# A graph layer's edge sums: gathers counted as landing later, and more sums fed to the matmul in two parts

## The chip, the cores and the metric

One core of a Trainium2 chip runs the whole kernel in one launch. The metric is the time of the device in microseconds (us); the median of three runs stands for a kernel. TensorE (PE) multiplies matrices and puts the result into PSUM, VectorE (DVE) and ScalarE (ACT) work on rows of 128 partitions, GpSimd (POOL) issues the gathers (indirect DMAs), and SyncE (SP) issues the plain DMAs. Each engine takes its instructions strictly in the order in which they were written; across engines they wait for one another by semaphores.

## The reference

A relational graph layer over 625 nodes of 512 features, 20625 edges sorted by destination, 4 kinds of edges. What matters, with the norms written as functions:

```python
h   = relu(layernorm(x))
msg = sum over r of (h[src] @ W_rel[r] + b_rel[r]) * where(type == r, weight, 0)
agg = segment_sum(msg, dst) / max(segment_sum(weight, dst), 1)
x1  = layer_norm(h + h @ W_self + b_self + agg)
out = x + layer_norm(x1 + gelu(x1 @ W_ffn1 + b_ffn1) @ W_ffn2 + b_ffn2)
```

All of it is float32. The kernel computes h @ W_rel[r] for all nodes and kinds first (the table), so that an edge's message is one row of the table, times its weight.

## The kernel before

The nodes lie in five blocks of 128 rows. The first 84 us make the table: 20 chunks of 128 rows (4 kinds by 5 blocks), each four float32 matmuls, stored to DRAM. The first and the last block (the outer ones) take their messages from dense products of the chunks with small matrices of summed weights; for that, chunks are loaded back from DRAM (L1297, SP) into three buffers of two chunks, and multiplied (L1302, PE). For the three inner blocks the rows are gathered edge by edge, and this is where the change lies.

A gather (L1159, POOL) fetches 128 rows of the table, one per partition, into one of ten buffers "ms". There are 99 of them. The first eight and the last one are single tiles, whose rows go straight to a matmul. The other 90 are 30 groups of three tiles in which the edges of one partition have the same destination, so the three rows can be added before the matmul: ScalarE takes the first row times its weight into one of two PSUM buffers "add" (L1165), VectorE adds the second and third (L1183). Then the group's sum goes to TensorE with a matrix of ones and zeros "oh" that picks the destination, and TensorE accumulates all groups of a run in "acc". Six further gathers (L1216, "x_row"), two for each inner block, fetch the edges of a node that share a group with the node before; VectorE adds them to the block's sums itself (L429). A run is the stretch of tiles that fall into the same block, or into the same two neighbours. By their groups the five runs with groups have 8, 2, 9, 2 and 9 of them; I number the groups 1 to 30 in this order. The last run also has the last single tile.

The sum of a group gets to TensorE in one of two ways. Whole: VectorE's last add writes it to a buffer "es", and TensorE multiplies it in float32 (L1208), which takes two passes. In two parts ("parted", or split): ScalarE casts the sum to a shorter format, "eh" (L1169), VectorE takes the rest, "el", by subtraction (L1173), and TensorE multiplies each in one fast pass (L1205, L1206).

When a run is complete, VectorE adds "acc" to the block's row sums z (L429); a block with all its parts is normalised (L880 to L892), turned by TensorE (L351) and copied by ScalarE (x1T, L1363). Then comes its feed-forward: eight up-projections (L928, 16 of the profile's matmul instructions for every two of them), each followed by a gelu on ScalarE (L932), eight down-projections (L946), the second norm on VectorE (L956 to L971, with root steps L862 to L869) and the store. The feed-forwards run in the order first outer, last outer, then the three inner blocks; by this order I speak of the fourth block (the second inner one) and of the last block (the third inner one). Self products of a block's own rows (L441) and sums over outer tiles (L613) fill in between. After the last run's sums TensorE may do dummy matmuls, the spins (L1226), at the lowest rank.

All of this, from the first gather on, is put into order by a planner (class Plan, L76). Each step is registered with an engine, a duration, the steps it comes after and the buffers it takes and gives back; the planner plays the steps through with these numbers and writes the instructions in the order in which they started in that play. Nothing else of the numbers reaches the chip. Two of them matter here. A gather takes 1.26 and counts as landed 3.6 (LAND) after that, plus an extra by its index n among the 99 gathers (LATE, L1258): the first pair of the table whose bound exceeds n gives the extra. And `parted` (L1175) says which groups go in two parts.

Of the kernel before, what the change touches and what calls it, by code (L numbers as in the profile page):

```python
# [154 lines left out]
def gnn_layer(ctx, tc, x, edges, edge_line, edge_groups, w_self, w_rel, w_ffn1, w_ffn2, rows_in, bf1_in, out, n_edges):  # L155
# [852 lines left out]
    SUM = 3  # L1008
    WARM = 24
    ES = 7  # L1010
    LAND, LATE = 3.6, ((8, 2.0), (40, 1.2))
    HOTS_AT, SELF_AT, ADDS_AT = (15, 16, 17), 15, (16, 17, 18)
    OHS = 3
    OW = 5
# [1 line left out]
    GATHER = 1.26  # L1016
    SLACK = 1.2
    LATER = 0.3
    PARTED = 1, 1
    BEHIND = 5  # L1020
    CELLS = 3.0
    FIRST_PIECE = 4
# [102 lines left out]
    order_of = sorted(of_sum, key=lambda bs: (not set(bs) & set(OUTER), -bs[0] if set(bs) & set(OUTER) else bs))  # L1125
# [37 lines left out]
    def first_row(j, ms, box):  # L1163
        box["sum"] = buffer("add")
        nc.scalar.activation(box["sum"], ms[j], AF.Copy, scale=wgt[:, j:j + 1])  # L1165

    def high(j, box):
        box["high"] = edge.tile([P, D], F32R, tag="es", name=f"eh_{j}", bufs=ES)
        nc.scalar.copy(box["high"], box["sum"])  # L1169

    def low(j, box):
        box["low"] = edge.tile([P, D], F32R, tag="es", name=f"el_{j}", bufs=ES)
        nc.vector.tensor_sub(box["low"], box["sum"], box["high"].bitcast(F32))  # L1173

    def parted(k, units):  # L1175
        return len(units[k]) > 1 and k % PARTED[1] < PARTED[0] and k + 3 < len(units)

    def row_added(j, ms, box, parts):
        k, q = divmod(j - GROUP0, EG)
        to = box["sum"]  # L1180
        if q == EG - 1 and not parts:
            to = edge.tile([P, D], F32, tag="es", name=f"es_{j}", bufs=ES)
        nc.vector.scalar_tensor_tensor(to, ms[j], wgt_g[:, k, q - 1:q], box["sum"], op0=ALU.mult, op1=ALU.add)  # L1183
        box["sum"] = to
# [46 lines left out]
    for bs in order_of:  # L1231
        tiles = of_sum[bs]
        units = []
# [13 lines left out]
        for k, unit in enumerate(units):  # L1247
# [15 lines left out]
            for q, (j, g) in enumerate(zip(unit, got)):  # L1263
                alone, whole = len(unit) == 1, q == len(unit) - 1
                if alone:
                    h = g
                elif q == 0:
                    h = row0 = op("ACT", 0.69, lambda j=j, box=box: first_row(j, ms, box), after=[g],
                                  take=["add"], give=[("ms", g)], lag=SLACK, rank=rank)
                else:  # L1270
                    parts = parted(k, units)
                    h = op("DVE", 0.75, lambda j=j, box=box, parts=parts: row_added(j, ms, box, parts), after=[g, h],
                           take=["es"] if whole and not parts else [],
                           give=[("ms", g)] + ([("add", row0)] if whole and not parts else []), lag=LATER, rank=rank)
                    h_last = h
                    if whole and parts:
                        h = op("ACT", 0.65, lambda j=j, box=box: high(j, box), after=[h], take=["es"], rank=rank)
                        h = op("DVE", 0.7, lambda j=j, box=box: low(j, box), after=[h], take=["es"], give=[("add", row0)], lag=0.6, rank=rank, level=0.7)
            end = unit is units[-1]
            parts = parted(k, units)  # L1280
            m = op("PE", 0.47 if parts else 0.87,
                   lambda bs=bs, k=k, q=k - k0, end=end, ohs=ohs, box=box, j=unit[0]: edge_sum(bs, k, q, end, ohs, box, j),
                   after=[h, hots_op, m], take=["acc"] if k == 0 else [],
# [290 lines left out]
```

## Time and profile before

| | |
|---|---|
| median of three runs | 260.74 us (260.15 to 263.15) |
| the profiled execution | 262.26 us, its span 260.5 us |
| granted TensorE clock, mean | 0.993 |
| busy: TensorE, VectorE, GpSimd, ScalarE | 95%, 77%, 66%, 29% of the span |
| gathers of L1159 | 99, the first at 88.1 us, the last at 221.7 us |

In a row of the timeline stand start, duration, engine, line, operation, what is written and read, the count, and in brackets the idle time of the engine just before, with what ended it. A float32 matmul is two instructions in the counts. The durations of neighbouring instructions overlap a little, since an engine begins one while the one before drains; where it matters, the time from start to start is used. In a group's row (a line, engine and operation) stand the count, the busy time, the mean in nanoseconds, and the idle time ahead. In a row by windows stand the stretch, its length, busy time and count of each engine in the order PE, weight loads, DVE, ACT, POOL, then granted clock, DMA share and GB/s.

### The profile page before, as it was taken

Reading aid. Unit: us, or ns where it says so; the run is one execution under the profiler, and the core shown is the slowest. Engines: PE = TensorE matmul, PEld = TensorE weight load, DVE = VectorE, ACT = ScalarE, POOL = GpSimd, SP = SyncE. Lnnn points to the kernel's source line nnn. Section 1 sums busy time; section 2 is a strip of 40 time slices with the busy share of each in tenths; the row PEclk is TensorE's granted clock in tenths of the full one; section 3 lists DMA queues with packets and bytes.
Section 4 is the critical chain, followed back from the end, with each engine's and each line's share of the span. In section 5 each row is a group of like instructions: output and inputs, shape, how many; then the busy total and the mean of one; then the engine's idle time right before and its main releaser. Section 6 shows DMA issues by size and latency. Waiting matters only on the chain. (4 is left out here: it accounts for less than half of the span.)

```text
span 260.5 us, 3515 instructions
## 1 busy us (share of the span) xinstructions
PE 246.4 (95%) x1051; PEld 141.4 (54%) x1051; DVE 200.5 (77%) x503; ACT 74.8 (29%) x224; POOL 172.0 (66%) x230
## 2 busy tenths in 40 slices
PE   8899999999999969999959999989999998899996
PEld 6444444445445625443424444864685964675964
DVE  2896999997979964839879399997798985973614
ACT  3017300000031573623121142641223632310420
POOL 4478889887888577777778777777777777100000
PEclk9999999999999999999999999999999999799999
DMA  5999999972272599799997977777776677330101
GB/s 191 361 402 416 379 382 360 321 285 81 73 253 85 199 363 328 227 346 299 367 325 219 374 232 201 218 191 208 213 212 205 199 204 213 111 110 6 44 0 44
DMA packets 24055, 60.20 MB, mean 231 GB/s; under 512 B 4401, under 2 KB 8753, under 8 KB 22882
## 3 DMA queue, kind: packets, MB, share of 16 engines
q0 software_dynamic: 9936, 27.58, 35.0%
q1 hardware_dynamic: 13808, 30.94, 32.1%
q10 hardware_dynamic: 290, 1.44, 1.6%
q8 instruction: 9, 0.15, 0.2%
q14 instruction: 12, 0.10, 0.1%
HBM read 50.77 MB, written 9.17 MB: 230 GB/s over the span
## 5 line engine op out<-in xcount | busy, mean ns | idle before, releaser
L1159 POOL DMA_INDIRECT ms<-table,row_i x99 | 97.2, 982 | 30.8 <-issue 13.4
L403 PE MATMUL ps<-wr,hT 128*128 128x512 f32 (+2 forms) x168 | 71.2, 576 | 0.0
L686 POOL DMA_INDIRECT cells<-weight,cell x45 | 48.6, 1080 | 9.0 <-issue 6.4
L403 PEld LDWEIGHTS ps<-wr,hT 128*128 128x128 f32 x168 | 30.6, 190 | 33.8 <-issue 29.9
L1183 DVE SCALAR_TENSOR_TENSOR add<-ms,wgt_g,add 128x512 f32<-128x512 f32 x48 | 35.7, 748 | 16.8 <-DMA ms<-table,row_i 14.9
L928 PEld LDWEIGHTS ps<-x1T,w_sb 128*128 128x128 f32 x320 | 39.1, 197 | 5.2 <-issue 3.2
L928 PE MATMUL ps<-x1T,w_sb 128*128 128x128 f32 (+1 forms) x320 | 39.7, 281 | 0.9 <-ACT gT L932 0.9
L1165 ACT ACTIVATE add<-ms,ed 128x512 f32<-128x512 f32 x30 | 20.7, 692 | 66.5 <-DMA ms<-table,row_i 47.3
L946 PE MATMUL ps<-w_sb,gT 128*128 128x512 f32 (+3 forms) x96 | 36.2, 522 | 0.0
L1302 PE MATMUL acc<-tr,sums_w 128*128 128x512 f32 x60 | 27.7, 595 | 0.0
L599 ACT ACTIVATE ohw<-os,w 128x128 fp32r<-128x128 f32 x36 | 11.4, 389 | 56.3 <-DVE os L581 55.3
L946 PEld LDWEIGHTS ps<-w_sb,gT 128*128 128x128 f32 (+1 forms) x96 | 16.6, 188 | 14.4 <-issue 11.8
L932 ACT ACTIVATE gT<-ps,bf 128x128 f32<-128x128 f32 (+1 forms) x40 | 13.3, 362 | 19.6 <-PE ps L928 14.9
L441 PE MATMUL ps<-ws_sb,hT 128*128 128x512 f32 x40 | 18.3, 592 | 0.0
L1302 PEld LDWEIGHTS acc<-tr,sums_w 128*128 128x128 f32 x60 | 11.0, 190 | 12.3 <-issue 11.2
L1208 PE MATMUL acc<-es,oh 128*128 128x512 f32 x24 | 12.9, 626 | 3.2 <-DVE es L1183 3.2
L416 DVE SCALAR_TENSOR_TENSOR tr<-ps,rx,brel_bc 128x512 f32<-128x512 f32 x15 | 11.2, 744 | 3.3 <-POOL idle L689 2.1
L1173 DVE TENSOR_TENSOR el<-add,eh 128x512 fp32r<-128x512 f32 x18 | 12.3, 681 | 0.9 <-ACT eh L1169 0.8
L1169 ACT CAST eh<-add 128x512 fp32r<-128x512 f32 x18 | 10.5, 581 | 8.2 <-DVE add L1183 8.2
L956 DVE TENSOR_TENSOR ow<-ps,z 128x512 f32<-128x512 f32 (+3 forms) x6 | 3.6, 599 | 11.4 <-PE ps L946 11.3
L441 PEld LDWEIGHTS ps<-ws_sb,hT 128*128 128x128 f32 x40 | 7.6, 190 | 8.7 <-issue 8.6
L1205 PE MATMUL acc<-eh,oh 128*128 128x512 f32 x18 | 11.7, 651 | 0.0
(215 smaller groups left out, 302.5 us busy)
## 6 DMA issues: line engine op xcount, KB each, us to landing
tr<-table SPq DMA_DIRECT2D x11, 512.0 KB, 6.3
w_sb<-in_L_gnn_W_ffn_dram SPq DMA_DIRECT2D x2, 2048.0 KB, 9.5
table<-tr SPq DMA_DIRECT2D x15, 256.0 KB, 6.3
wr<-in_L_gnn_W_rel_dram SPq DMA_DIRECT2D x3, 1024.0 KB, 8.8
cells<-zeros SPq DMA_DIRECT2D x2, 1280.0 KB, 12.5
ms<-table,row_i POOLq DMA_INDIRECT x99, 3.8
rows<-in_rows_dram SPq DMA_DIRECT2D x1, 1536.0 KB, 13.0
sums_w<-cells ACTq DMA_DIRECT2D x1, 1280.0 KB, 5.9
```

Of the source, the lines that this page charges most:

```text
L403: nc.tensor.matmul(p_[:, :h.stop - h.start], hT[i][:, k, :], wr_sb[r][:, k, h], start=(k == 0), stop=(k == KD - 1))
L441: nc.tensor.matmul(p[0], hT[i][:, k, :], ws_sb[:, k, :], start=(k == 0), stop=(k == KD - 1))
L686: s = nc.gpsimd.indirect_dma_start(out=cells[i][:, :], out_offset=bass.IndirectOffsetOnAxis(ap=cell[i][:, k:k + 1], axis=0), in_=weight[i] ...
L928: nc.tensor.matmul(pu[:, :nn], w1_sb[:, k, f * P:(f + 1) * P], x1T_b()[:, k, :nn], start=(k == 0), stop=(k == KD - 1))
L932: nc.scalar.activation(box["gT"][:, f, :nn], pus[f][:, :nn], AF.Gelu, bias=bf1[:, f:f + 1])
L946: nc.tensor.matmul(po[h][:n, :w], box["gT"][:, f, at], w2_sb[:, f, c], start=(f == 0), stop=(f == KF - 1))
L1159: nc.gpsimd.indirect_dma_start(out=ms[j], out_offset=None, in_=table[:, :], in_offset=bass.IndirectOffsetOnAxis(ap=row_i[:, j:j + 1], axis=0))
L1165: nc.scalar.activation(box["sum"], ms[j], AF.Copy, scale=wgt[:, j:j + 1])
L1173: nc.vector.tensor_sub(box["low"], box["sum"], box["high"].bitcast(F32))
L1183: nc.vector.scalar_tensor_tensor(to, ms[j], wgt_g[:, k, q - 1:q], box["sum"], op0=ALU.mult, op1=ALU.add)
L1208: nc.tensor.matmul(acc[bs], ohs[0][:, q, :].bitcast(F32), box["sum"] if "sum" in box else ms[j], start=(k == 0), stop=last)
L1302: nc.tensor.matmul(acc[b,], sums_w[b][:, c, :], kept[(b, c) if (b, c) in kept else c], start=first, stop=last)
```

## The change

Two settings of the layout, and the rule for split sums:

```diff
-    LAND, LATE = 3.6, ((8, 2.0), (40, 1.2))
+    LAND, LATE = 3.6, ((8, 3.5), (56, 2.5), (120, 0.5))
...
-    PARTED = 1, 1
+    PARTED = 2, 3
...
-    def parted(k, units):
-        return len(units[k]) > 1 and k % PARTED[1] < PARTED[0] and k + 3 < len(units)
+    def parted(bs, k, units):
+        return len(units[k]) > 1 and k % PARTED[1] < PARTED[0] and (k + 3 < len(units) or bs != order_of[-1])
...
-                    parts = parted(k, units)
+                    parts = parted(bs, k, units)
...
-            parts = parted(k, units)
+            parts = parted(bs, k, units)
```

LATE: the first eight gathers now count as landing 3.5 later than LAND instead of 2.0, those up to the 40th 2.5 instead of 1.2, those from there to the 56th 2.5 instead of nothing, and the rest, up to the 99th, 0.5 instead of nothing. The x_row gathers keep LAND alone.

PARTED: before, every group is split, other than the last three members of its run. Now the first two of every three groups of a run are split, and the last three members are left whole only in the last run (bs is the run's blocks, order_of[-1] the last run).

Both change the order that the planner writes out. Three places follow, on which the prediction rests.

TensorE, near the end of the first run of groups (the fifth to eighth group's sums, into acc_1); before:

```order
L1205 MATMUL acc_1_1174<-eh_1229,oh_1190 128x512
L1206 MATMUL acc_1_1174<-el_1263,oh_1190 128x512
L1208 MATMUL acc_1_1174<-es_1244,oh_1190 128x512
L1208 MATMUL acc_1_1174<-es_1277,oh_1190 128x512
L351 MATMUL ps_81<-ident,ow_954 128x128 x4
L1302 MATMUL acc_1234<-tr_3_1226,sums_w_984 128x512
L1208 MATMUL acc_1_1174<-es_1296,oh_1190 128x512
L1302 MATMUL acc_1234<-tr_3_1226,sums_w_984 128x512
L1302 MATMUL acc_1234<-tr_5_1246,sums_w_984 128x512 x2
L1302 MATMUL acc_1234<-tr_7_1275,sums_w_984 128x512 x2
L441 MATMUL ps_80<-ws_sb,hT_147 128x512 x2
```

The same place now (the reloaded chunks are the tiles tr, the self products L441):

```order
L1302 MATMUL acc_1236<-tr_3_1219,sums_w_984 128x512 x2
L441 MATMUL ps_80<-ws_sb,hT_147 128x512 x2
L351 MATMUL ps_81<-ident,ow_954 128x128 x4
L1302 MATMUL acc_1236<-tr_5_1258,sums_w_984 128x512 x2
L441 MATMUL ps_80<-ws_sb,hT_147 128x512 x2
L1205 MATMUL acc_1_1170<-eh_1281,oh_1192 128x512
L1206 MATMUL acc_1_1170<-el_1310,oh_1192 128x512
L1205 MATMUL acc_1_1170<-eh_1306,oh_1192 128x512
L1206 MATMUL acc_1_1170<-el_1313,oh_1192 128x512
L1302 MATMUL acc_1236<-tr_7_1277,sums_w_984 128x512 x2
L1302 MATMUL acc_1236<-tr_9_1289,sums_w_984 128x512 x2
```

The run's last two sums, groups 7 and 8, were whole and are split now, and they have moved behind the rest of tr_3, all of tr_5 and the second half of the self product.

VectorE, at the first two x_row gathers of the third run (z<-ms,x_on); before:

```order
L429 SCALAR_TENSOR_TENSOR z<-ps_78,rx,rows 64x512
L429 SCALAR_TENSOR_TENSOR z<-ps_78,rx,z 64x512
L1183 SCALAR_TENSOR_TENSOR es_1572<-ms_948,wgt_g,add_83 128x512
L429 SCALAR_TENSOR_TENSOR z<-ms_952,x_on,z 128x512
L429 SCALAR_TENSOR_TENSOR z<-ms_943,x_on,z 128x512
L1183 SCALAR_TENSOR_TENSOR add_82<-ms_944,wgt_g,add_82 128x512
```

The same place now:

```order
L868 SCALAR_TENSOR_TENSOR rs_z_1402<-rs_z_1402 128x1
L869 SCALAR_TENSOR_TENSOR rs_z_1402<-rs_z_1402 128x1
L429 SCALAR_TENSOR_TENSOR z<-ms_949,x_on,z 128x512
L1183 SCALAR_TENSOR_TENSOR add_82<-ms_948,wgt_g,add_82 128x512
L429 SCALAR_TENSOR_TENSOR z<-ms_950,x_on,z 128x512
L1183 SCALAR_TENSOR_TENSOR es_1585<-ms_952,wgt_g,add_82 128x512
L1173 TENSOR_TENSOR el_1592<-add_83,eh_1571 128x512
```

The first x_row operation stood behind the last group of the run (es_1572); now it stands ahead of both adds of that group (add_82, es_1585) and ahead of the rest el of the group before.

TensorE, at the last sums of the last run (es, then the single tile's ms), with the fourth block's up-projections (L928) and down-projections (L946); before:

```order
L1205 MATMUL acc_1_1701<-eh_1849,oh_1726 128x512
L1206 MATMUL acc_1_1701<-el_1852,oh_1726 128x512
L1208 MATMUL acc_1_1701<-es_1860,oh_1726 128x512
L928 MATMUL ps_78<-x1T_1752,w_sb 128x128 x4
L928 MATMUL ps_81<-x1T_1752,w_sb 128x128 x4
L928 MATMUL ps_80<-x1T_1752,w_sb 128x128 x4
L1208 MATMUL acc_1_1701<-es_1891,oh_1844 128x512
L1208 MATMUL acc_1_1701<-ms_951,oh_1874 128x512
L928 MATMUL ps_79<-x1T_1752,w_sb 128x128 x4
L928 MATMUL ps_78<-x1T_1752,w_sb 128x128 x4
L928 MATMUL ps_81<-x1T_1752,w_sb 128x128 x4
L946 MATMUL ps_80<-w_sb,gT_1855 128x512 x4
```

The same place now, from the eighth and last of the up-projections on:

```order
L928 MATMUL ps_81<-x1T_1832,w_sb 128x128 x4
L1205 MATMUL acc_1_1730<-eh_1877,oh_1779 128x512
L1206 MATMUL acc_1_1730<-el_1897,oh_1779 128x512
L1208 MATMUL acc_1_1730<-es_1890,oh_1779 128x512
L946 MATMUL ps_79<-w_sb,gT_1850 128x512 x2
L1208 MATMUL acc_1_1730<-es_1929,oh_1883 128x512
L1208 MATMUL acc_1_1730<-ms_947,oh_1911 128x512
L946 MATMUL ps_79<-w_sb,gT_1850 128x512 x6
L351 MATMUL ps_78<-ident,ow_957 128x128 x2
L351 MATMUL ps_80<-ident,ow_957 128x128 x2
L1226 LDWEIGHTS zeros
L1226 MATMUL spin<-zeros 128x256
```

Before, six of the eight up-projections and all down-projections stood behind the sum of group 28; now all eight stand ahead of it, and two of the down-projections ahead of group 30's. Five spins have come in ahead of the last block's up-projections; 25 are left at the end.

## The prediction

> **What bounds the kernel now.** I read the page first, then the gathers on POOL, the chain of waits, TensorE's idle gaps, and its clock by windows.
>
> ```profile
> span 260.5 us, 3515 instructions
> PE 246.4 (95%) x1051; PEld 141.4 (54%) x1051; DVE 200.5 (77%) x503; ACT 74.8 (29%) x224; POOL 172.0 (66%) x230
> 209.10 0.95 POOL L1159 DMA_INDIRECT ms<-table,row_i  x1 [0.30 <-DVE mv_y L331]
> ...
> 221.72 0.94 POOL L1159 DMA_INDIRECT ms<-table,row_i  x1 [0.30 <-DVE add L1183]
> DMA to landing us min/median/max: 3.6/3.8/6.6
> ```
>
> Two things run without rest. TensorE is busy for 95% of the span. POOL starts a gather every 1.26 us (ten between the two rows) and idles the same 0.30 us before each, so it never waits for a buffer; its last gather starts at 221.72 us and lands, at the median, near 225.5. Which of the two sets the end is told by the chain (start, us, what):
>
> ```profile
> 222.22 0.67 DVE es L1183
> ...
> 222.93 1.52 PE acc L1208 x2
> 224.45 3.93 PE ps L928 x24
> 228.38 1.72 PE acc L1208 x4
> 230.09 2.68 PE ps L928 x24
> 232.77 3.44 PE ps L946 x8
> 236.21 0.44 PE ps L351 x4
> 236.65 3.44 PE ps L946 x8
> 240.08 7.14 PE ps L928 x64
> 247.23 6.95 PE ps L946 x32
> ```
>
> From 222.93 to 254.17 it is TensorE's queue alone. When the last gather has landed, three quarters of the fourth block's up-projection (48 of 64 L928) and its whole down-projection (L946) are still undone; the last block's 64 L928 begin at 240.08. So TensorE is late because it idled while gathers were under way:
>
> ```profile
> 94.57 1.10 PE L1208 MATMUL acc<-ms,oh 128*128 128x512 f32 x2 [1.82 <-issue]
> ...
> 136.73 1.12 PE L1208 MATMUL acc<-es,oh 128*128 128x512 f32 x2 [3.03 <-DVE es L1183]
> ...
> 163.56 1.95 PE L928 MATMUL ps<-x1T,w_sb 128*128 128x128 f32 x16
> ...
> 173.47 0.66 PE L351 MATMUL ps<-ident,ow 128*128 128x128 f32 x4 [0.88 <-DVE z L429]
> ...
> 218.35 1.95 PE L928 MATMUL ps<-x1T,w_sb 128*128 128x128 f32 x16
> ...
> 222.28 0.49 PE L1206 MATMUL acc<-el,oh 128*128 128x512 f32 x1 [1.74 <-DVE el L1173]
> 134.00:135.00 1.00, 0.00 (x0) 0.00 (x0) 0.49 (x1) 0.00 (x0) 0.83 (x1) 1.00 1.04 381
> ...
> 225.00:226.00 1.00, 1.00 (x7) 1.00 (x7) 0.97 (x4) 0.00 (x0) 0.00 (x0) 0.50 0.00 0
> ```
>
> These gaps are 7.5 us. The last two rows are one-microsecond windows; third from the end stands the granted clock. It stays 1.00 in the gap of 3.03 us but is 0.50 after that of 1.74 us: the 24 L928 took 3.93 us against 2.68 for the next 24, and two L1208 1.52 against 0.86, so 1.9 us went to the clock.
>
> **The change, part by part.** *Two of three sums in two parts.* A run has 8, 2, 9, 2 and 9 groups of three. Before, 5+0+6+0+7 = 18 are split; now 6+2+6+2+5 = 21.
>
> ```profile
> 143.70 1.02 PE L1208 MATMUL acc<-es,oh 128*128 128x512 f32 x2
> 144.56 1.88 PE L441 MATMUL ps<-ws_sb,hT 128*128 128x512 f32 x4
> ...
> 154.46 1.02 PE L1302 MATMUL acc<-m,sums_w 128*128 128x512 f32 x2
> 154.91 0.80 PE L1205 MATMUL acc<-eh,oh 128*128 128x512 f32 x1
> 155.55 0.39 PE L1206 MATMUL acc<-el,oh 128*128 128x512 f32 x1
> 155.78 1.88 PE L1302 MATMUL acc<-m,sums_w 128*128 128x512 f32 x4
> L1173 DVE TENSOR_TENSOR el<-add,eh 128x512 fp32r<-128x512 f32 x18 | 12.3, 681 | 0.9 <-ACT eh L1169 0.8
> ```
>
> From start to start a whole sum holds TensorE 0.86 us; a split one holds it 155.78 - 154.46 - 0.86 = 0.46. Three more splits save 1.2 us of TensorE; each costs VectorE one L1173 (0.68, 2.0 in all) and ScalarE one cast, which its 29% hides. VectorE, busy 77%, hides them in its waits for gathers; without that cover they cost up to 2.0 us once.
>
> *Gathers counted as landing later.* No work is added; every in-order queue is rearranged.
>
> ```profile
> ms<-table,row_i POOLq DMA_INDIRECT x11, 5.5
> ...
> ms<-table,row_i POOLq DMA_INDIRECT x12, 3.7
> 134.51 0.75 DVE L429 SCALAR_TENSOR_TENSOR z<-ms,x_on,rows 64x512 f32<-64x512 f32 x1 [1.89 <-DMA ms<-table,x_row]
> 135.27 0.74 DVE L429 SCALAR_TENSOR_TENSOR z<-ms,x_on,z 64x512 f32<-64x512 f32 x1
> 135.94 0.73 DVE L1183 SCALAR_TENSOR_TENSOR es<-ms,wgt_g,add 128x512 f32<-128x512 f32 x1
> ```
>
> The first two rows are issue to landing for gathers issued from 115 to 130 us and from 190 to 205: the early ones, beside the 512 KB reloads of table rows, take about 1.8 us longer. At three places this decides.
>
> First, near 92.75 us TensorE idles 1.82 us. Now two other sums and an outer block's matmul stand ahead; but the next gathered rows land at the same times, so I credit only 0.4 us.
>
> Second, at 133.7 us. In the new order more reloaded chunks and half of a self product (five matmuls, 4.3 us) go ahead of the blocking sums. VectorE still waits to 134.51 for the x_row gather, then has five row operations (0.67 to 0.76 from start to start, 3.4 in all), a mask (I take 0.3) and two splits (1.4) to do, to 139.6. TensorE, which turns the first block at about 132.3 as before, has 0.9 of transposes and 3.4 of matmuls behind that, so it arrives at 136.6 and resumes after both splits, at 139.9. Before, the blocking sum ended at 136.73 + 0.86 = 137.6. The lead is 137.6 + 4.3 - 139.9 = 2.0 us. From there 22 matmuls of 0.86 and four splits lead to the first up-projection: 139.9 + 18.9 + 1.8 = 160.6, against the row at 163.56, a lead of 2.9. The eight ups (7.14), two splits and a transpose (0.6) end at 169.2; before, the row at 173.47, with its gap of 0.88, leads to the same work at 173.8 (173.47 + 0.5 for it + 0.89 for the last up, less a transpose and a split that the new order has later): a lead of 4.6. Then gathers hold it: VectorE, now early, comes to the x_row operation near 174.6 and waits 3.8 us for its gather (started near 174.7, 3.7 to land), and TensorE 1.4 us for the split behind. That wait is new; behind it on VectorE stand two adds and that split, and it only eats lead.
>
> Third, the tail. All eight up-projections of the fourth block now stand ahead of the last three sums, the down-projection behind them. TensorE's work from 169.2 to there is 24 downs of 0.86, 16 ups of 0.89, eight splits, four whole sums and two transposes, 43 us; with the wait of 1.4 it gets there near 213.6. Group 27's last gather (row 209.10) lands at 212.9, its add ends at 213.6 too, and its sum at 214.5. From there:
>
> ```profile
> 215.48 5.30 DMA ms<-table,row_i
> 231.48 0.74 DVE L429 SCALAR_TENSOR_TENSOR z<-acc,rdeg,z 128x512 f32<-128x512 f32 x1
> ...
> 235.02 0.88 DVE L892 SCALAR_TENSOR_TENSOR ow<-ow,rs_z,rows 128x256 f32<-128x256 f32 x2 [0.47 <-POOL rs_z L344]
> 236.46 0.65 ACT L1363 COPY x1T<-ps 128x256 f32<-128x256 f32 x2 [2.12 <-PE ps L351]
> ```
>
> Eight ups 7.14, plus 1.0 behind a gelu that queues after a row product of group 29: 222.7. The gather at 215.48 lands at 220.8 again; VectorE's two adds, small work and split end at 223.4, and two sums and two downs end at 226.0. Group 30's second add ends at 227.0, its sum at 227.9, the single tile's at 228.8, the six downs left (0.86 each) at 233.9. VectorE meanwhile has four pairs of root steps (1.3) and two L971 (1.3), so z starts at 229.6; z to x1 is 4.4 us in the rows less one L971 that now lies ahead, so x1 is there at 233.4. Transposes 0.44, copies 0.65: the last up-projection starts at about 235.2 against 240.08. Five spins (0.72, from 257.06 to 257.78 in the chain) that now precede it lie inside the copies' time.
>
> ```profile
> 257.06 0.72 PE spin L1226 x5
> ```
>
> Behind it nothing changes. **Sum:** -4.9, rounded to -4.7 for the waits I can't see. By the profiled execution's own time (262.26, its span plus 1.8) that is 257.6. That execution lies 1.5 above the median of 260.74, so on the median: 256.0.
>
> Bounds of the forecast: if every sum at the end comes right at its landing (225.3, 226.2, then 0.86 each), the up-projection starts at 233.5, -6.5. If the lead is lost and TensorE reaches the eight ups at 218.35 as before, 7.14 + 0.46 + 0.86 + 1.72 + 1.72 + 5.16 + 0.44 + 0.72 bring it to 236.6, still -3.5, because work stands where the gap and the half clock were.
>
> One rule bears on the half clock. The Trainium skill, page "TensorE: Matmul & The Clock Gate", section "Why this matters for your kernels", asks for no idle gap over about 3 us, one idle window bringing half the clock. By it none of the gaps left in my tail (1.0 us at most) would halve the clock, and the sum stands; the rows disagree both ways (3.03 us without, 1.74 us with), and the rows decide.
>
> **The rivals.**
> - *The half clock comes back in the tail.* Three gaps of about 1 us remain between 218 and 227. For: 1.74 us sufficed. Against: gaps of 0.88 near up-projections at 173.47 did not. Price 1.9, in the ups or downs: -2.8, so 257.9. Chance 0.12.
> - *The idle only changes its name.* TensorE waits as long, for splits behind x_row gathers on a VectorE that has 2.0 us more to do, and reaches the ups near 221.3, 3 us later than before. For: VectorE is the releaser in three of the gaps above. Against: its own waits leave room. Then about 239.5: -0.6, 260.1. Chance 0.13.
> - *Slower: gathers stop for buffers.* Ten ms buffers at 1.25 us are 12.5 us. Near 136.7 my walk consumes the tile gathered at 126.25, 10.4 us on, behind VectorE's wait for x_row. If that gather lands over 2.1 us later (reloads moved earlier beside it), POOL stalls and all later gathers shift one for one. With a shift of 7.5 us the time is 263.5; slower by 1% it is from a stall of 7.3 us. Against: POOL's rows show no such wait. Chance 0.08.
>
> That the change does nothing is excluded by the order.
>
> **How the numbers follow.** The forecast has 0.67, from 254.2 to 257.2. About 1% (2.6 us) is what a measurement of this kernel can tell from no change. Faster by more: 0.67 and two thirds of the clock's case, 0.75. Within: the rest of it and the renamed idle, 0.17. Slower: 0.08. The range runs from 254.0 (best bound) to 259.6, which leaves out the slower case and most of the renamed idle.
>
> **What would show it.** Right: 21 L1205 and 9 whole L1208 sums; no gap near 92.75; the gap at 133.7 smaller and later; first L928 near 160.6; POOL still 1.25 us per gather; the last 64 L928 start near 235.2 at clock 1.00. Wrong: a POOL idle over 0.30, a first L928 not before 163, a half clock after 218, or VectorE's z later than 231.

## The result and the profile after

The changed kernel takes 260.03 us (median of 20 runs, 256.95 to 263.07) against 261.82 for the one before in the same series (20 runs, 259.64 to 263.45), 1.8 us faster by the medians. The ratio is 0.990 (0.988 to 0.993), or 2.5 us, since it leaves out, as all ratios below do, the runs over 1.5% above the fastest of their kernel, here eight of the changed one's twenty. I had forecast 256.0, 4.7 us faster, and a range up to 259.6. The direction is right, the gain at most about half. The forecast also started from 260.74, a median of three runs that lies 1.1 us under that of these twenty.

The page of the changed kernel's profiled run (261.25 us), its last gather on POOL, TensorE's longest idle times (in brackets) and two windows of one microsecond (TensorE's busy time, then the granted clock):

```profile
span 259.5 us, 3522 instructions
PE 245.8 (95%) x1051; PEld 141.4 (55%) x1051; DVE 201.6 (78%) x505; ACT 76.8 (30%) x227; POOL 172.3 (66%) x230
222.81 0.95 POOL L1159 DMA_INDIRECT ms<-table,row_i  x1 [0.30 <-issue]
95.60 2.08 PE L1208 MATMUL acc<-ms,oh 128*128 128x512 f32 x4 [1.14 <-issue]
139.77 0.50 PE L1206 MATMUL acc<-el,oh 128*128 128x512 f32 x1 [2.34 <-DVE el L1173]
140.71 5.29 PE L1302 MATMUL acc<-tr,sums_w 128*128 128x512 f32 x8
221.26 5.47 PE L928 MATMUL ps<-x1T,w_sb 128*128 128x128 f32 x32 [2.01 <-ACT gT L932]
237.45 7.31 PE L928 MATMUL ps<-x1T,w_sb 128*128 128x128 f32 x64
142.00:143.00 1.00, 1.00 (x2) 0.50 0.83 258
224.00:225.00 1.00, 1.00 (x7) 0.50 0.76 221
```

The gap of 1.82 us near 92.75 is down to 1.14, those ahead of 173.47 and 222.28 are gone, and the last up-projections start 2.6 us sooner (237.45 against 240.08). Of those over 2 us two are left, 2.34 and 2.01, the second in a new place, and behind each stands half a clock: eight L1302 took 5.29 us, 32 L928 5.47. But 2.6 us sooner there is only 1.0 sooner at the end of the span. Behind the last up-projections, VectorE's last row and the landing of the three stores on SP's queue, of the kernel before:

```profile
256.48 0.88 DVE L971 SCALAR_TENSOR_TENSOR ow<-ow,rs_y,xs 128x320 f32<-128x320 f32 x2
DMA to landing us min/median/max: 1.7/1.8/2.0
```

and of the changed one:

```profile
254.01 0.88 DVE L971 SCALAR_TENSOR_TENSOR ow<-ow,rs_y,xs 128x320 f32<-128x320 f32 x2
DMA to landing us min/median/max: 2.0/3.2/3.3
```

From the end of VectorE's last row to the end of the span are 260.5 - 257.36 = 3.1 us before and 259.5 - 254.89 = 4.6 now. So there are three suspects: the wait of 2.01 us, the half clock, and a last store that lands 1.5 us later.

### The profile page after: what moved, and what is told of

It is laid out like the page before. It is cut to its first block, busy times and chain, and to the rows that moved or that the text cites. A ratio compares the mean times of both kernels' runs of the same rounds, so it can differ in the third digit from the quotient of the medians.

```text
span 259.5 us, 3522 instructions
## 1 busy us (share of the span) xinstructions
PE 245.8 (95%) x1051; PEld 141.4 (55%) x1051; DVE 201.6 (78%) x505; ACT 76.8 (30%) x227; POOL 172.3 (66%) x230
## 4 chain that ended last, share of the span: by engine, by line
PE 58%; DMA 23%; DVE 10%; issue 3%; POOL 2%; SPq 1%; ACT 1%; POOLq 0%; DVEq 0%; ACTq 0%
PE ps L403 25%; DMA ms<-table,row_i 16%; PE acc L1302 8%; PE ps L928 7%; PE ps L946 5%; DMA ms<-table,x_row 4%; PE acc L1208 4%; DVE add L1183 3%; PE ps L441 3%; DMA wr<-in_L_gnn_W_rel_dram 3%; POOL ms L1159 2%; DVE z L429 2%; PE ps L613 2%; PE spin L1226 2%; DVE el L1173 1%
## 5 line engine op out<-in xcount | busy, mean ns | idle before, releaser
L1183 DVE SCALAR_TENSOR_TENSOR add<-ms,wgt_g,add 128x512 f32<-128x512 f32 x51 | 38.0, 748 | 5.9 <-DMA ms<-table,row_i 3.3
L928 PEld LDWEIGHTS ps<-x1T,w_sb 128*128 128x128 f32 x320 | 38.8, 199 | 4.9 <-ACT gT L932 2.4
L928 PE MATMUL ps<-x1T,w_sb 128*128 128x128 f32 (+1 forms) x320 | 39.2, 283 | 2.0 <-ACT gT L932 2.0
L946 PE MATMUL ps<-w_sb,gT 128*128 128x512 f32 (+3 forms) x96 | 36.2, 522 | 0.0
L1302 PE MATMUL acc<-tr,sums_w 128*128 128x512 f32 x60 | 29.6, 626 | 0.0
L946 PEld LDWEIGHTS ps<-w_sb,gT 128*128 128x128 f32 (+1 forms) x96 | 16.6, 188 | 14.5 <-issue 11.8
L441 PE MATMUL ps<-ws_sb,hT 128*128 128x512 f32 x40 | 18.6, 592 | 0.0
L1302 PEld LDWEIGHTS acc<-tr,sums_w 128*128 128x128 f32 x60 | 11.6, 199 | 12.6 <-issue 11.7
L1169 ACT CAST eh<-add 128x512 fp32r<-128x512 f32 x21 | 12.3, 584 | 18.4 <-DVE add L1183 17.0
L1173 DVE TENSOR_TENSOR el<-add,eh 128x512 fp32r<-128x512 f32 x21 | 14.1, 680 | 3.3 <-ACT eh L1169 3.3
L1205 PE MATMUL acc<-eh,oh 128*128 128x512 f32 x21 | 13.3, 632 | 0.0
L441 PEld LDWEIGHTS ps<-ws_sb,hT 128*128 128x128 f32 x40 | 7.6, 190 | 8.0 <-issue 7.7
L1206 PE MATMUL acc<-el,oh 128*128 128x512 f32 x21 | 8.8, 420 | 2.7 <-DVE el L1173 2.6
## 6 DMA issues: line engine op xcount, KB each, us to landing
table<-tr SPq DMA_DIRECT2D x15, 256.0 KB, 6.2
```

Of the source, the lines that this page charges most:

```text
L441: nc.tensor.matmul(p[0], hT[i][:, k, :], ws_sb[:, k, :], start=(k == 0), stop=(k == KD - 1))
L928: nc.tensor.matmul(pu[:, :nn], w1_sb[:, k, f * P:(f + 1) * P], x1T_b()[:, k, :nn], start=(k == 0), stop=(k == KD - 1))
L946: nc.tensor.matmul(po[h][:n, :w], box["gT"][:, f, at], w2_sb[:, f, c], start=(f == 0), stop=(f == KF - 1))
L1205: nc.tensor.matmul(acc[bs], ohs[0][:, q, :], box["high"], start=(k == 0), stop=False)
L1302: nc.tensor.matmul(acc[b,], sums_w[b][:, c, :], kept[(b, c) if (b, c) in kept else c], start=first, stop=last)
```

## The experiments

Ten of the eighteen runs fell on chips on which every kernel, the one before too, took about 20% longer (the one before 309.6 to 325.8 us); the nine ratios on record have intervals of 0.5 to 1.2% to either side, and their profiles can't be laid beside the others (the 99 gathers alone take 158 to 166 us there from the first issue to the last, against 133 to 135). They stand with their kernels, and the reading goes by the runs on the other chips. Their profiles:

| kernel | last gather issued | last 64 L928 start | VectorE's last row ends | span | ratio to before, interval |
|---|---|---|---|---|---|
| before | 221.72 | 240.08 | 257.36 | 260.5 | 1 |
| changed | 222.81 | 237.45 | 254.89 | 259.5 | 0.990 (0.988 to 0.993) |
| after_quiet (changed) | 222.69 | 235.90 | 253.34 | 258.3 | 0.992 (0.989 to 0.995) |
| late_alone_quiet | 222.66 | 237.91 | 255.35 | 258.5 | 0.995 (0.992 to 0.999) |
| parted_alone_again | 222.64 | 237.38 | 254.82 | 257.9 | 0.991 (0.987 to 0.994) |
| held_quiet | 220.75 | 233.60 | 251.05 | 256.4 | 0.991 (0.988 to 0.995) |
| gelus_first_again | 222.63 | 234.91 | 252.35 | 256.4 | 0.987 (0.982 to 0.992) |
| gelus_first_direct | 222.63 | 234.14 | 251.58 | 255.6 | 0.988 (0.985 to 0.992) |
| spins_last | 221.99 | 235.47 | 253.02 | 256.3 | 0.987 (0.982 to 0.991) |
| gelus_spins | 221.36 | 233.90 | 251.45 | 254.6 | 0.978 (0.975 to 0.982) |

Each profile is of one execution. The changed kernel and after_quiet are the same program, and their spans differ by 1.2 us; with the change in the kernel the last gather is issued anywhere from 220.75 to 222.81, though POOL idles no longer than before. So a difference of a microsecond between two profiles is not yet one between their kernels.

### Each part alone

The later landings alone (against the changed kernel):

```diff
-    PARTED = 2, 3
+    PARTED = 1, 1
-        return ... and (k + 3 < len(units) or bs != order_of[-1])
+        return ... and k + 3 < len(units)
```

> The later landings alone; splits as in the kernel before (18). Theory P (each part pays by itself: the due times close TensorE's waits, the splits take 1.2 us off TensorE): about half of the gain is left, ratio to before 0.995 (0.993 to 0.998). Rival Q (the gathers hold the end, so waits closed before 175 us are waited for again later): ratio 0.998 to 1.003, with the gaps near 95, 137 and 174 us as small as in the changed kernel all the same.

> The later landings alone (18 split sums as before), again, since all kernels were slowed on the chip of its first call. Theory P (each part pays by itself): ratio 0.993 to 0.998. Rival Q (the landings' part is waited for again at the gathers; the splits and the order of the last block carry the gain, as parted_alone_again at 0.9905 says): ratio 0.998 to 1.003, the last 64 up-projections at 239.5 to 240.5 us where the tail's clock is the same as before, though the gap near 137 us is smaller than 3.0.

> The later landings alone (18 split sums as before), since the chips of the two calls before took some 20 % longer for every kernel. Theory P (each part of the change pays by itself): ratio 0.993 to 0.998. Rival Q (the landings' part is waited for again at the gathers, and the splits with the order of the last block carry the gain): ratio 0.998 to 1.003; the gap near 137 us smaller than 3.0, yet the last 64 up-projections at 239 to 240.5 us.

The splits alone:

```diff
-    LAND, LATE = 3.6, ((8, 3.5), (56, 2.5), (120, 0.5))
+    LAND, LATE = 3.6, ((8, 2.0), (40, 1.2))
```

> The 21 split sums alone; landings counted as in the kernel before. Theory P: the splits' 1.2 us of TensorE show in full or nearly, ratio 0.995 to 0.997, gaps of 1.8 us near 95 and 3.0 us near 137 as before. Rival Q: the end is set by the gathers and the order of the last block, so the ratio depends on the tail alone: 0.990 if the first four up-projections of the fourth block stand ahead of its last groups' sums as in the changed kernel, 1.000 if not.

> The same kernel as parted_alone. Theory P (each part of the change pays by itself): the splits' 1.2 us of TensorE show nearly in full, ratio 0.995 to 0.997. Rival Q (waits closed before 175 us are waited for again at the gathers, and the order of the last block decides): 0.990 if the fourth block's first up-projections stand ahead of its last groups' sums as in the changed kernel, 1.000 if not.

Measured: the landings 0.995 (on the slower chips 0.992, 0.986 to 0.998, and 0.984, 0.976 to 0.991), the splits 0.991 (there 0.991, 0.986 to 0.996). TensorE in late_alone_quiet:

```profile
139.22 1.12 PE L1208 MATMUL acc<-es,oh 128*128 128x512 f32 x2 [2.56 <-DVE es L1183]
237.91 7.31 PE L928 MATMUL ps<-x1T,w_sb 128*128 128x128 f32 x64
```

and in parted_alone_again, with the landings counted as before the change:

```profile
137.67 1.88 PE L1302 MATMUL acc<-tr,sums_w 128*128 128x512 f32 x4
140.51 0.66 PE L351 MATMUL ps<-ident,ow 128*128 128x128 f32 x4 [0.96 <-DVE ow L892]
237.38 7.31 PE L928 MATMUL ps<-x1T,w_sb 128*128 128x128 f32 x64
```

For the landings theory P's number is the measured one (rival Q's band, from 0.998, touches the interval's edge). For the splits it is Q's: 0.990, and Q's condition holds, since four of the fourth block's up-projections stand ahead of the sum of group 28 in that profile. P had allowed them 0.995 to 0.997, or 1.2 us, and they bring 2.5. With them the gap of 3.03 us near 137 shrinks to 0.96 without any later landing, while the landings alone leave 2.56 of it; how much of the 2.5 is this gap and how much the order at the end was not separated. If the two simply added, 0.995 x 0.991 = 0.986, they would give 3.7 us. The changed kernel's 0.990 is a microsecond short of that, a difference within the intervals. One thing sets it apart from both parts in every profile: they end 3.1 to 3.2 us behind VectorE's last row, it ends 4.6 to 5.1 behind.

### The half clock

Products of zeros fill the two gaps:

```diff
+    def hold(p, n):
+        for _ in range(n):
+            nc.tensor.matmul(p[:, :D // 2], zeros[:, D // 2:D // 2 + P], zeros[:, D // 2:], start=False, stop=False)
...
+            if bs == (1,) and k in (6, 7):
+                hold(acc[bs], 14 if k == 6 else 2)
             nc.tensor.matmul(acc[bs], ohs[0][:, q, :], box["low"], start=False, stop=last)
...
+                        (lambda up=up: (spin(14), up())) if f == 4 and blocks == together[-2] else up,
```

> The changed kernel with 16 products of zeros added to the accumulating sum in the 2.34 us gap near 138 us, and 14 products of zeros between the fourth and the fifth up-projection of the fourth block (2.01 us gap near 220 us); 0.146 us each, so they fill the gaps without lengthening them, and add nothing to any sum. Theory C (half clock after gaps is part of the loss, and differs from run to run by the gaps' phase): mean clock 0.997 to 1.000 in every run, none under 0.993, scatter of the times smaller, median 1.5 to 3 us under the changed kernel's, ratio 0.980 to 0.985. Rival B (the gathers hold the end, the clock's loss lies in time that is waited anyway): clock up as said, ratio 0.988 to 0.993.

> The changed kernel with products of zeros in its two gaps (16 near 138 us, 14 between the fourth and the fifth up-projection of the fourth block), again. Theory C (the half clock after these gaps is part of the loss): clock 0.997 to 1.000 in nearly every run, against 0.985 to 1.000, median 1 to 2.5 us under after_again's. Rival B (time that is waited anyway): clock up, median within 0.7 us of after_again's.

> The changed kernel with products of zeros in its two gaps (16 near 138 us, 14 between the fourth and the fifth up-projection of the fourth block), for the same reason again. Theory C (the half clock after these gaps is part of the loss): clock 0.997 to 1.000 in nearly every run, ratio 0.980 to 0.986. Rival B (it falls into time that is waited anyway): clock up, ratio 0.988 to 0.993.

Measured: mean clock 0.995 to 1.000 in all twelve runs, and yet 0.991, the ratio of the changed kernel (on the slower chips 0.998, 0.989 to 1.008, and 0.987, 0.978 to 0.996). TensorE in held_quiet, the filled place in the tail (L1232 is the line of the products of zeros in that kernel) and the last up-projections:

```profile
217.62 1.69 PE L1232 MATMUL spin<-zeros 128*128 128x256 bf16 x14
219.15 3.74 PE L928 MATMUL ps<-x1T,w_sb 128*128 128x128 f32 x32
233.60 7.31 PE L928 MATMUL ps<-x1T,w_sb 128*128 128x128 f32 x64
```

The 32 up-projections take 3.74 us there, not 5.47. So the clock was held, and the ratio is rival B's; theory C's 0.980 to 0.986 lies outside the interval. (In this run the row came early, so the products took some of the time that they were to fill; I can't exclude that this hid up to a microsecond.) The runs of the kernel before tell the size without any edit. In the 67 of them on the other chips whose clock is on record, its mean clock is 1.00, 0.993, 0.987 or 0.980, which is none to three stretches of half a clock: by windows of half a microsecond both stretches of the changed kernel's profile last 3.4 us, and one takes 3.4 x 0.5 / 260 = 0.0066 off the mean. The mean times are 261.3, 261.9, 262.2 and 262.7 us. So a stretch that takes 5.29 - 3.59 = 1.7 us of TensorE's time (140.71 here, 140.49 in after_quiet) costs on average some 0.5 us (0.2 to 0.7 by a straight line through the 67) at the end.

That is an average over wherever the stretches fall. In the tail one costs nearly its whole length: the second half of the fourth block's up-projections starts at 221.26 in the changed kernel's profile and at 221.34 in after_quiet, and only the first has the half clock behind it; the last up-projections start at 237.45 and 235.90, 1.55 us apart. The 32 runs of the changed kernel (these twenty and after_quiet's twelve) give 1.0 us for each 0.0066 of clock by such a line, 0.4 to 1.6. So the half clock is part of the changed kernel's loss in the runs that have it in the tail; what holding it is worth in the median, up to about a microsecond, the intervals leave open.

### The wait of the fifth up-projection

ScalarE works in order. In the changed kernel, run again as after_quiet, its queue, and TensorE's rows beside it:

```profile
215.11 0.69 ACT L1165 ACTIVATE add<-ms,ed 128x512 f32<-128x512 f32 x1 [1.75 <-DMA ms<-table,row_i]
220.31 0.69 ACT L1165 ACTIVATE add<-ms,ed 128x512 f32<-128x512 f32 x1 [4.51 <-DMA ms<-table,row_i]
220.94 0.61 ACT L932 ACTIVATE gT<-ps,bf 128x128 f32<-128x128 f32 x2
215.62 3.73 PE L928 MATMUL ps<-x1T,w_sb 128*128 128x128 f32 x32
221.34 3.84 PE L928 MATMUL ps<-x1T,w_sb 128*128 128x128 f32 x32 [1.99 <-ACT gT L932]
235.90 7.31 PE L928 MATMUL ps<-x1T,w_sb 128*128 128x128 f32 x64
215.13 5.09 DMA ms<-table,row_i
```

The planner put the product of group 29's first row (220.31) ahead of the fourth block's first gelu (220.94). It did not count that row as landing too soon after its gather: by its numbers it lands 1.26 + 3.6 + 0.5 = 5.36 us after the gather starts, and here it took 5.09 (last line, from the chain). Which of its other times made the product come first in the play is not shown. ScalarE stands still for 4.51 us, four up-projections fill the four ps tiles, and the fifth waits 1.99. The edit lets the planner see the first rows of groups 29 and 30 (with the single tile the last three members of the run) 2.5 us later on ScalarE alone:

```diff
-                    h = row0 = op("ACT", 0.69, lambda j=j, box=box: first_row(j, ms, box), after=[g],
+                    seen = g if bs != order_of[-1] or k + 3 < len(units) else op("x1", 0.0, None, after=[g], lag=2.5)
+                    h = row0 = op("ACT", 0.69, lambda j=j, box=box: first_row(j, ms, box), after=[seen],
```

> The changed kernel, but in the planner's view the gathered rows of the last three groups of the last run reach ScalarE 2.5 us later, so that the first two gelus of the fourth block stand ahead of the row product of the second-last group in ScalarE's queue. Theory A (the loss against the forecast is the 2.0 us wait of the fourth up-projection behind that row product and the half clock after it): no gap over 0.6 us between the fourth block's up-projections, no half clock between 220 and 227 us, the last 64 up-projections begin at 235.0 to 236.0 instead of 237.45, ratio 0.980 to 0.985. Rival B (the last gathers hold the end): the gap moves to the wait for the second-last group's sum, the last 64 begin at 237 to 238, ratio 0.988 to 0.993.

> The same kernel as gelus_first, since all kernels took some 20 % longer on the chip of that call. Theory A (the loss against the forecast is the 2.0 us wait of the fourth block's up-projections behind the row product of the second-last group, and the half clock after it): no gap over 0.6 us between them, no half clock from 220 to 227 us, the last 64 up-projections begin at 235.0 to 236.0 instead of 237.45, ratio to before 0.980 to 0.985. Rival B (the last gathers hold the end): the gap moves to the wait for the second-last group's sum, the last 64 begin at 237 to 238, ratio 0.988 to 0.993.

> The changed kernel unaltered, as the direct measure for gelus_first_direct: ratio 0.988 to 0.993. Theory T (the end is the last gather's issue and the work that is still ahead of TensorE then): 35 to 37 us from the issue of the last gather to the end of the span, with a wait of 1.5 to 2.5 us of the fifth up-projection of the fourth block.

> The changed kernel with the last three groups' row products behind the first two gelus on ScalarE, beside the changed kernel on one chip. Theory T: 33.5 to 34.5 us from the last gather's issue to the end, median 1.5 to 2.8 us under after_quiet's, ratio 0.980 to 0.986. Rival B (the wait only moves): 35 us or more, median within 0.8 us of after_quiet's.

Two gelus now stand ahead of that product, and in gelus_first_direct all up-projections of the fourth block run through:

```profile
215.50 7.35 PE L928 MATMUL ps<-x1T,w_sb 128*128 128x128 f32 x64
234.14 7.31 PE L928 MATMUL ps<-x1T,w_sb 128*128 128x128 f32 x64
```

The wait is gone, as theory A's mechanism has it, and the last ones start at 234.14 against 235.90. In gelus_first_again 0.55 us of the wait is left. But the ratios of the two series are 0.987 and 0.988 (on the slower chip 0.988, 0.977 to 1.000), where A wanted 0.980 to 0.985, and side by side the medians are 258.45 us against 259.58, 1.1 apart, between theory T's 1.5 to 2.8 and rival B's 0.8 or less. The profiles show more, spans of 255.6 against 258.3: 1.8 us up to the last up-projections and 1.0 behind VectorE's last row (4.0 us to the end here, 5.0 in after_quiet, where the store landed after 3.8). From the last gather's issue to the end are 33.0 us here and 35.6 in after_quiet (T: 33.5 to 34.5, and 35 to 37). The profiles flatter the edit, since the profiled execution here, 257.5 us, is the fastest of its six, while after_quiet's, 260.12, lies above its median. So the wait is shown, and its worth in the median, about a microsecond with what was won behind VectorE's last row, is less than A said.

### The closing products

The kernel ends TensorE's queue with 30 products of zeros (L1226). In the changed one the planner found a free place for five of them ahead of the last up-projections, so 25 are left behind the last matmul; in gelus_first 20. In both kernels with one part alone all 30 are at the end. This edit puts them there in the changed kernel and moves nothing else:

```diff
-            if bs == order_of[-1] and k + SPINS >= len(units):
-                for _ in range(3 if end else 1):
-                    op("PE", 0.55, lambda: spin(5), after=[m], take=["one"], give=["one"], rank=rank, level=9)
...
+    for _ in range(SPINS + 2):
+        op("PE", 0.55, lambda: spin(5), after=[down_last], take=["one"], give=["one"], rank=(0, n), level=9)
```

> The changed kernel with all thirty closing products of zeros after the last down-projection again (five of them stood ahead of the last 64 up-projections); no other instruction moves. Theory F (TensorE runs out of instructions 0.7 us sooner, and the load of the code that follows meets the last store): the last store lands in 1.7 to 1.9 us, not 3.3 to 3.8, VectorE's last row to the end of the span takes 3.1 us, not 4.6 to 5.0, and the median falls 1.3 to 2 us, ratio to before 0.983 to 0.987. Rival G (the landing scatters by chance, or the store waits for something else): landing and ratio as in the changed kernel, 0.990 to 0.993.

> The same, with the last three groups' row products behind the fourth block's first two gelus on ScalarE as in gelus_first. If the two losses add up (theory F and theory A): no wait over 0.6 us between the fourth block's up-projections, last store landed in 1.7 to 1.9 us, ratio 0.978 to 0.983, which is the forecast's size or more. If F fails: 0.987 to 0.989, as gelus_first.

The DMA queues from the issue of the last two stores on (queue, kind: packets, MB, share of 16 engines; then each store's KB and us to landing), in the changed kernel from 254.0 to 256.7 us:

```profile
q1 hardware_dynamic: 270, 0.25, 26.4%
q8 instruction: 1, 0.02, 2.9%
q14 instruction: 1, 0.01, 0.8%
out_dram<-ow SPq DMA_DIRECT2D x1, 160.0 KB, 3.3
out_dram<-ow SPq DMA_DIRECT2D x1, 96.0 KB, 3.2
```

and in spins_last from 252.2 to 254.6 (the load on q8 follows at 254.7):

```profile
q1 hardware_dynamic: 288, 0.26, 31.7%
q14 instruction: 1, 0.01, 1.0%
out_dram<-ow SPq DMA_DIRECT2D x1, 160.0 KB, 1.8
out_dram<-ow SPq DMA_DIRECT2D x1, 96.0 KB, 1.9
```

With 25 products a load of instructions on q8 falls among the packets of the stores (at 255.75), 18 of the 288 come later than the window, and the store lands after 3.3 us; with 30 all 288 are through ahead of the load, and the two land after 1.8 and 1.9. TensorE's last products, in spins_last, the changed kernel and gelus_first_direct, end at 254.18, 255.30 and 251.23:

```profile
249.66 4.52 PE L1226 MATMUL spin<-zeros 128*128 128x256 bf16 x30
251.54 3.76 PE L1226 MATMUL spin<-zeros 128*128 128x256 bf16 x25
248.23 3.00 PE L1226 MATMUL spin<-zeros 128*128 128x256 bf16 x20
```

In all ten profiles of the table above the load on q8 comes 0.3 to 0.6 us behind the end of TensorE's last product, so it is TensorE's queue that sets it off. The profiles of all runs, those on the slower chips too, sort by the number of products left behind the last matmul:

| products behind | profiles | VectorE's last row to the end of the span | the 160 KB store lands after (ten profiles above) | the load comes (the same ten) |
|---|---|---|---|---|
| 30 | 10 | 3.1 to 3.3 us | 1.8 us | behind the stores' packets |
| 25 | 6 | 4.6 to 5.4 us | 3.3 to 4.1 us | among them |
| 20 | 4 | 4.0 to 4.2 us | 2.5 us | just ahead of them |

So theory F holds, and the profiles price it at 1.3 to 2.3 us. Why so small a load delays the last packets that long is not shown. The median gives 0.987 (F: 0.983 to 0.987; G: 0.990 to 0.993), 0.9 us below the changed kernel by the two ratios, where F had 1.3 to 2; the intervals overlap, and the landings are the plainer proof. With all 30 at the end the two parts of the change add up: 0.987 against the 0.986 of their product. The Trainium skill, page "Runtime: NRT & Kernel Launch", section "Instruction fetch mechanics", says that the sequencer refills its instructions in blocks of 16 KiB by a DMA queue of its own and that the cost of crossing into the next block is mostly hidden. The row of q8, one packet of 0.02 MB, agrees on such a load, and here it was not hidden.

TensorE and the store in gelus_spins:

```profile
220.89 2.05 PE L928 MATMUL ps<-x1T,w_sb 128*128 128x128 f32 x16 [1.15 <-ACT gT L932]
233.90 7.41 PE L928 MATMUL ps<-x1T,w_sb 128*128 128x128 f32 x64
DMA to landing us min/median/max: 1.7/1.8/2.0
```

It takes 256.18 us against 262.12, ratio 0.978, 5.9 us faster than the kernel before, and is the best of the kernels tried. The store lands as expected; a wait of 1.15 us, over the 0.6 expected, is left in this run. By the ratios this is some 1.5 us more than the two edits bring alone (from 0.990 to 0.987 each), and the profile doesn't explain the surplus: it ends 33.2 us behind the issue of its last gather, gelus_first_direct 33.0, and its last gather is issued 1.3 us sooner, which the place of the closing products doesn't touch.

### What stays open

> The changed kernel unaltered, as the measure for the others of this call: 0.988 to 0.993. If the two waits of the tail are of the order of the queue and not of chance, the wait of the fifth up-projection of the fourth block is again 1.5 to 2.5 us; if the half clock is a matter of phase, it stands in some other place or not at all.

> The 21 split sums with the landings of the kernel before, and the last three groups' row products counted 2.5 us later on ScalarE as in gelus_first. Theory R (the landings' part has a worth of its own that shows once the tail is unblocked): 1 to 2 us slower than gelus_first, ratio 0.991 to 0.995. Rival Q (the landings' part is worth nothing; splits and tail order make all of it): the same as gelus_first, ratio 0.983 to 0.989, the last 64 up-projections at 234.5 to 236.

> gelus_spins with the landings of the kernel before (8 gathers 2.0 us later, then to the 40th 1.2 us). Theory S (what is won before the last gathers is waited for again; splits, gelus and the closing products make the gain): ratio within 0.003 of gelus_spins, 0.975 to 0.981. Rival R (the landings are worth 1 to 2 us of their own): 0.982 to 0.988.

The x_row gathers' landing, in gelus_spins_x:

```diff
-                                take=["ms"], lag=LAND, order=True, rank=(0, n))
+                                take=["ms"], lag=LAND + next((late for most, late in LATE if n < most), 0.0), order=True, rank=(0, n))
```

> gelus_spins with the x_row gathers counted as landing later too, as the other gathers of their time are. Theory S: the gap near 137 us falls from 2.4 to under 1 us and the first up-projection comes 1 to 2 us sooner, but the last gather still is issued near 222.6 us and the ratio stays at 0.975 to 0.981. Rival R: the 1 to 2 us show, ratio 0.970 to 0.974.

All four fell on the slower chips: after_again 0.987 (0.979 to 0.995), without the wait of the fifth up-projection, since TensorE reaches the first one at 273.09 there, behind the last gather (269.58); gelus_old_late 314.87 us against 318.97, which is rival Q's size, with no interval; gelus_spins_old 0.976 (0.972 to 0.981); gelus_spins_x 0.989 (0.984 to 0.994). gelus_spins_old speaks for theory S, that the landings are worth nothing once the end is unblocked, but on a chip where the gathers take 160 us and not 134. gelus_spins_x is worse than either theory had it, there. Neither was tried on the other chips, so the worth of the landings beside the rest stays open.

## Why the prediction was right, and where it failed

1. *Two of three sums in two parts.* 21 splits, as counted. VectorE's busy time rose from 200.5 to 201.6 us; whether its waits hid all of that was not separated. The term of 1.2 us was mis-sized: alone the splits bring 2.5, in a run where the gap near 137 us shrank from 3.03 to 0.96. I had given that gap to the landings. How much of the 2.5 it is was not separated.
2. *The first place, near 92.75.* Credited with 0.4; the idle of 1.82 fell to 1.14, and to 0.72 in after_quiet. "No gap" was too much.
3. *The second place.* In after_quiet, without half a clock there, the walk is found again:

```profile
140.49 3.59 PE L1302 MATMUL acc<-tr,sums_w 128*128 128x512 f32 x8
161.22 6.41 PE L928 MATMUL ps<-x1T,w_sb 128*128 128x128 f32 x56
169.73 3.60 PE L946 MATMUL ps<-w_sb,gT 128*128 128x512 f32 x8
178.37 0.75 DVE L429 SCALAR_TENSOR_TENSOR z<-ms,x_on,z 128x512 f32<-128x512 f32 x1 [3.55 <-DMA ms<-table,x_row]
```

   I had 139.9, 160.6 and 169.2, and VectorE's wait of 3.8 from 174.6 on, measured 3.55 from 174.8. And as I said, the gathers then eat into the lead. In the profiled run of the changed kernel the half clock at 141 us moved the first up-projection to 163.15, which made the sign "not before 163" look met, and that at 223 us the sign of z (231.52 there, 229.96 in after_quiet): a sign that one run can give by its clock alone is a poor sign.
4. *The tail.* The eight up-projections start at 215.51 (forecast 214.5); the last gather was issued 1.1 us later than before, without any idle over 0.31 on POOL; other profiles of kernels with the change have it at 220.75 to 222.69, so that this is the change's doing is not shown. The step "plus 1.0 behind a gelu that queues after a row product" named the mechanism and mis-sized it: 2.01, 1.99 and 2.29 us (in spins_last). My own figures held more: four up-projections from 214.5 are done at 218.1, and the row that ScalarE waits for was put at 220.8. With the wait cut to 1.15 us and without point 5 the gain is 5.9 us (gelus_spins), more than the forecast's 4.7.
5. *"Behind it nothing changes."* This is the step that failed. I saw the five products move, costed them where they now stand (hidden in the copies, which is right but for 0.14 us: from the last transposes to the up-projections are 0.98 us, 0.84 in spins_last) and not where they are missing. There they had kept a load of instructions behind the last store: 4.6 and 5.0 us from VectorE's last row to the end instead of 3.1 in the two profiles, 0.9 us in the medians. In after_quiet, whose clock is whole, this is most of the miss: the last 64 up-projections start 0.7 us later than forecast (235.90 against 235.2), and the span ends 2.7 us later than the 260.5 - 4.9 = 255.6 of the sum, 1.9 of it behind VectorE's last row.
6. *The rivals.* The half clock did come back in the tail of the profiled run (0.50 at 224 us) and was absent in after_quiet (mean clock 0.999); in that run it cost 1.55 of the 1.9 that I took from TensorE's rows. A stretch anywhere in the kernel before costs about 0.5 on average. The Trainium skill, page "TensorE: Matmul & The Clock Gate", section "Why this matters for your kernels", asks for gaps under about 3 us; gaps of 2.34 and 2.01 us were followed by half the clock here, one of 1.99 was not, so the rows decide against the rule. The idle that only changes its name gave the measured number, 260.1, by a mechanism that the profile doesn't show: TensorE reached the up-projections at 215.5, not at 221.3. POOL never stopped for buffers.

## What to carry to other kernels

An instruction that is moved leaves a place too: cost what it did where it stood, above all for fillers at the end of a queue, where the next load of code can meet the last store. On an engine that works in order, an operation on a late DMA must not stand ahead of a short one that another engine waits for; look for the largest idle time whose releaser is a DMA and read what is queued behind it. And a loss of clock or a gap is worth in the total what it costs at the next thing that is waited for, here 0.5 us of 1.7 on average, but 1.55 in the tail, where TensorE's queue alone sets the end.

## What the runs showed of the hardware

- A store of 160 KB at the end landed after 1.8 us with one load of instructions of 0.02 MB behind its packets, after 2.5 us with the load just ahead of them, and after 3.3 to 4.1 us with the load among them, though that load took only 2.9% of the DMA engines' time in the piece of the changed kernel.
- That load came 0.3 to 0.6 us behind the end of TensorE's last product in all ten profiles of the table.
- A gap of 3.03 us left the clock at 1.00 in the kernel before, while gaps of 2.34 and 2.01 us were followed by 0.50 for 3.4 us in one run of the changed kernel, and one of 1.99 us by no loss in another.
- The kernel before took about 262 us on some chips and 310 to 326 on others; the profiled runs there had mean clocks of 0.91 to 0.93.
